# Two selective-scan layers of a Trainium2 kernel: another order of the four scan directions, the last image's norm cut into row blocks beside the last scans, part of the first image's convolution moved beside the first scans

## The chip, the cores and the metric

The kernel runs on one core of a Trainium2 chip. The metric is the device time of one execution in microseconds (us); the time before is the median of three runs. The names of the engines are those of the profile: PE is the matrix engine (PEld its weight loads), DVE the vector engine, ACT the scalar engine, POOL the GpSimd engine, SP the engine whose queue issues the DMAs.

## The reference, cut to what matters

Four layers work on 8 images of 48 x 48 pixels with 96 channels, each as `x = x + layer(groupnorm(x))`. The first and the last layer (L0 and L3) are the ones that the change touches. Both compute this:

```python
xz = x @ in_proj.T;  xc, z = split(xz)               # 2 x 192 channels
xc = silu(depthwise_conv3x3(xc))
xs = [rows forward, columns forward, rows backward, columns backward] of xc
for each of the 4 directions: dts, B, C = x_proj @ xs;  delta = softplus(dt_proj @ dts + bias)
    h = exp(delta * A) * h + (delta * u) * B          # 192 channels x 16 states, 2304 steps
    y = sum over the states of h * C + D * u
y = the four directions' y, put back to pixels and added
y = (y - mean) / sqrt(var + 1e-5) * norm_w + norm_b   # over the 192 channels of a pixel
out = (y * silu(z)) @ out_proj.T
```

A pixel's norm needs all four directions of that pixel, and nothing of other pixels. The second layer is a spectral filter with a small network, the third another scan layer; the change leaves their work as it is.

## The kernel before, in words

`ss2d` is one such layer. The 2304 pixels are cut into five blocks, `BLKS`: four of 10 rows (480 pixels) and one of 8 rows (384). In a column direction the same numbers mean columns. Its parts are, in order of the program:

* `load_x(0)`, `front(0)`, `conv(0)`: the first image is loaded into the padded tile `xpad`, normed, and convolved. `conv(b)` takes, for each block and each half of the 192 channels, nine matmuls from `xpad` into the PSUM tile of tag `side` (L481), one matmul for z into a PSUM tile of tag `s1` (L486), then two Silu activations on ACT (L490 into `us[b]`, L492), and stores z to `zs[b]` in DRAM (L494). Before the scans nothing lies beside it.
* `scans`: 8 images x 4 directions x 5 blocks. A block is four *turns*. A turn is three pairs of scans on DVE (L263), with what feeds and reads them: exp(delta A) by ACT into PSUM (L255), delta u B by DVE and POOL (L235), h C by POOL (L276, about 3 us each, twice a turn), and the sum over the states by PE (L296, L298, function `reduce`). Twice in a turn `aside(at)` issues work that belongs to something else: loads for the next block, one step of the generator `side`, and a step of `stage1`, which prepares the block two ahead (L593, L583, L587, L598, L611, and L422 on POOL). An image has 160 asides: 20 blocks x 4 turns x 2.
* `opening` and `done`: the sum of the four directions is held in `yss`. A block starts its PSUM accumulation with what is there and writes it back (ACT, L634).
* `side(job)`: during the scans of image `job` it issues, a step per aside, `load_x` of the next image, the norm of the last image, `post(job - 1)` (from the fourth aside on, for 52 asides), `front` of the next image, and from aside 80 on `conv(job + 1)`, 80 steps.
* `post(b)` first takes for all five blocks mean (PE, L504), difference (DVE, L507), square (ACT, L510), its sum (PE, L515) and a copy to `var` (DVE, L518); then one square root (ACT, L520) and one reciprocal (DVE, L522) over all; then for each block the loads of z and x (L528, L530), the factor spread over the channels (PE, L534), two products (DVE, L538), the product with z (POOL, L541), the output product (PE, L544 and L547), the sum (DVE, L550) and the store (L552). After the scans `post(nb - 1)` does it for the last image with nothing beside it.

Each engine takes its instructions in the order in which the program issues them; this order is written out by hand (`manual_schedule`), and the framework only adds the waits. The directions run in the order 0 to 3, where the last one, 3, goes over columns from behind:

```python
DIRS_SS = [(False, False), (True, False), (False, True), (True, True)]   # (columns, backward)
```

Of the kernel before, what the change touches and what calls it, by code (L numbers as in the profile page):

```python
# [9 lines left out]
F32 = mybir.dt.float32  # L10
AF = mybir.ActivationFunctionType
# [4 lines left out]
H, W, C = 48, 48, 96  # L16
L = H * W
DH = 96
NS = 16
NK = 4  # L20
# [4 lines left out]
BLKS = [(0, 10), (10, 10), (20, 10), (30, 10), (40, 8)]  # L25
BMAX = 480
WMAX = BMAX + 1
NG = 8
# [10 lines left out]
CH = 96  # L39
# [36 lines left out]
def vss_stack_kernel(ctx: ExitStack, tc: tile.TileContext, i: dict, out: bass.AP):  # L76
# [86 lines left out]
        yield  # L163


    def scans(dirs, restart, a, pools, ps, stage1, opening, done, side, tail):

# [3 lines left out]


        blocks = [Block(job, k, blk, n == 0, n == len(BLKS) - 1, dirs[k][1])
                  for job in range(nb) for k in range(NK)
                  for n, blk in enumerate(range(len(BLKS))[::-1 if dirs[k][1] else 1])]
        for b in blocks:
            b.columns(restart)
# [168 lines left out]
        for t, (b, q) in enumerate(turns):  # L348
            at, nblk = 2 * t, t // (NG // 2)
            if q == 0:  # L350
                if nblk + 2 < len(blocks):
                    plan(blocks[nblk + 2], at)
                if b.k == 0 and b.first:
                    beside = side(b.job)
            scan(t, 0)
            if t > 0:
                keep(t - 1, 1)
                make_hc(t - 1, 1)
            make_dbu(at + 2, nc.vector)
            make_da(t, 1)  # L360
            make_dbu(at + 3, nc.gpsimd)
            if t > 0:
                reduce(t - 1, 0)
            scan(t, 1)
            make_da(t, 2)
            copy_b(at + 3)
            make_dbu(at + 3, nc.vector)
            if t > 0:
                reduce(t - 1, 1)
            aside(at)  # L370
            bring(t + 1)
            keep(t, 0)
            make_hc(t, 0)
            make_da(t + 1, 0)
            scan(t, 2)
            copy_b(at + 4)
            finish(at + 1)
            aside(at + 1)
            if q == NG // 2 - 1 and b.k == NK - 1 and b.last:
                for _ in beside:  # L380
                    while tail:
                        tail.pop(0)()
# [47 lines left out]
    def ss2d(l, xin, xout, b0=0):  # L430
# [36 lines left out]
        def load_x(b):  # L467
            nc.sync.dma_start(xpad[:C, 1:1 + H, 1:1 + W], seq(xin[b], False))

        def conv(b):  # L470
            us[b] = big.tile([DH, 2, L], F32, tag="big", name="u")
            zs[b] = zdr.tile([DH, 2, L], F32, tag="z", name="zd")
            for r0, nr in BLKS:
                n = nr * SEG
                for half in range(2):
                    pu = side_psum()
                    for slot in range(7):
                        for tap in ((0,), (1, 2), (3,), (4, 5), (6,), (7, 8), ())[slot]:
                            dy, dx = tap // 3, tap % 3
                            at = (2 * tap + half) * DH  # L480
                            nc.tensor.matmul(pu[:, :n], lhsT=flat[:, at:at + P],  # L481
                                             rhs=xpad[:, r0 + dy:r0 + dy + nr, dx:dx + W],
                                             start=(tap == 0), stop=(tap == 8))
                        if slot == 6:
                            pz = ps("s1", 1)
                            nc.tensor.matmul(pz[:DH, :n], lhsT=w[f"{l}_in"][:, (2 + half) * DH:(3 + half) * DH],  # L486
                                             rhs=xpad[:C, 1 + r0:1 + r0 + nr, 1:1 + W], start=True, stop=True)
                        yield
                    s = slice(r0 * W, r0 * W + n)
                    nc.scalar.activation(us[b][:, half, s], pu[:DH, :n], AF.Silu, bias=w[f"{l}_cb"][:, half:half + 1])  # L490
                    z = zp.tile([DH, BMAX], F32, tag="z", name="z")
                    nc.scalar.activation(z[:, :n], pz[:DH, :n], AF.Silu)  # L492
                    yield
                    nc.sync.dma_start(zs[b][:, half, s], z[:, :n])  # L494

        def post(b):
            y = yss[b]
            var = small.tile([CH, L // CH], F32, tag="var", name="var")
            for r0, nr in BLKS:
                n = nr * SEG  # L500
                s = slice(r0 * W, r0 * W + n)
                pm = side_psum()
                for half in range(2):
                    nc.tensor.matmul(pm[:DH, :n], lhsT=mean, rhs=y[:, half, s], start=(half == 0), stop=(half == 1))  # L504
                yield
                yc = y[:, :, s]
                nc.vector.tensor_sub(yc, yc, pm[:DH, :n].unsqueeze(1).to_broadcast([DH, 2, n]))  # L507
                yield
                sq = lnp.tile([DH, 2, BMAX], F32, tag="sq", name="sq", bufs=1)
                nc.scalar.activation(sq[:, :, :n], yc, AF.Square)  # L510
                yield
                pv = side_psum()
                for c in range(n // CH):
                    for half in range(2):
                        nc.tensor.matmul(pv[:CH, c:c + 1], lhsT=sq[:, half, c * CH:(c + 1) * CH], rhs=ones,  # L515
                                         start=(half == 0), stop=(half == 1))
                yield
                nc.vector.tensor_copy(var[:, r0 * W // CH:(r0 * W + n) // CH], pv[:CH, :n // CH])  # L518
                yield
            nc.scalar.activation(var, var, AF.Sqrt, bias=eps5[:CH])  # L520
            yield
            nc.vector.reciprocal(var, var)  # L522
            yield
            for r0, nr in BLKS:
                n = nr * SEG
                s = slice(r0 * W, r0 * W + n)
                z = lnp.tile([DH, 2, BMAX], F32, tag="zin", name="zin", bufs=1)
                nc.sync.dma_start(z[:, :, :n], zs[b][:, :, s])  # L528
                xi = xio.tile([C, BMAX], F32, tag="xi", name="xi")
                nc.sync.dma_start(xi[:, :n], xin[b][:, s])  # L530
                pr = side_psum()
                for c in range(n // CH):
                    at = r0 * W // CH + c
                    nc.tensor.matmul(pr[:DH, c * CH:(c + 1) * CH], lhsT=var[:, at:at + 1].to_broadcast([CH, DH]),  # L534
                                     rhs=wc["ident"], start=True, stop=True)
                yield
                for half in range(2):
                    nc.vector.scalar_tensor_tensor(y[:, half, s], y[:, half, s], w[f"{l}_nw"][:, half:half + 1], pr[:DH, :n],  # L538
                                                   ALU.mult, ALU.mult)
                yield  # L540
                nc.gpsimd.tensor_mul(y[:, :, s], y[:, :, s], z[:, :, :n])  # L541
                po = side_psum()
                for half in range(2):
                    nc.tensor.matmul(po[:C, :n], lhsT=wnb[:, half, :], rhs=z[:, half, :n], start=(half == 0), stop=False)  # L544
                yield
                for half in range(2):
                    nc.tensor.matmul(po[:C, :n], lhsT=w[f"{l}_out"][:, half, :], rhs=y[:, half, s],  # L547
                                     start=False, stop=(half == 1))
                yield
                nc.vector.tensor_add(xi[:, :n], xi[:, :n], po[:C, :n])  # L550
                yield
                nc.sync.dma_start(xout[b][:, s], xi[:, :n])  # L552

        def side(job):
            used = 0
            more = job + 1 < nb
            if more:
                load_x(job + 1)
            if job > 0:

                for _ in range(3):
                    used += 1
                    yield
                for _ in post(job - 1):
                    used += 1
                    yield
            if more:
                for _ in front(job + 1):
                    used += 1
                    yield  # L570
                while used < 10 * NG:
                    used += 1
                    yield
                yield from conv(job + 1)

        def stage1(b):
            n = b.n
# [60 lines left out]
        load_x(0)  # L638
        for _ in front(0):
            pass  # L640
        for _ in conv(0):
            pass
        scans(dirs, False, a, pools, ps, stage1, opening, done, side, [])
        for _ in post(nb - 1):
            pass
        stack.close()

# [1 line left out]
    def lines(xin, xout):  # L649
# [169 lines left out]
        load_x(0)  # L819
        for _ in front(0):  # L820
            pass
        scans(dirs, True, a, pools, ps, stage1, opening, done, side, tail)
        stack.close()


# [286 lines left out]
```

## Time and profile before

| | us |
|---|---|
| median of 3 runs (19544.21 to 19555.11) | 19550.73 |
| the profiled execution | 19542.61 |
| its span, first to last instruction | 19540.6 |
| L0: start to the first scan | 148.7 |
| L0: after the last scan to the last sum of the norm | 5902.6 to 6007.1 |
| L3: start of the layer to its first scan | 13528.4 to 13675.7 |
| L3: after the last scan to the end | 19432.6 to 19540.6 |
| a 10-row block in L0 and L3 with nothing beside it | 34.5 to 34.8 |
| an 8-row block in L0 and L3 with nothing beside it | 29.5 to 31.5 |

A block's time is the distance from its first scan to the first scan of the next block, read from the scans (L263) in the trace's timeline of DVE. In the views, each row of a timeline has start, duration, engine, line, operation and operands, and in brackets how long the engine stood idle before it and for what. A windows view gives the busy time and the count of instructions of each engine in a stretch, the clock granted to PE as a share, the busy share of the DMA engines, and GB/s. All stretches of time are us from the start of the span.

### The profile page before, as it was taken

How to read it: one execution, taken by the hardware profiler on the slowest of the kernel's cores; microseconds unless marked ns; L12 is line 12 of the kernel's file. 1: busy time of each engine (PE TensorE's matmuls, PEld its weight loads, DVE VectorE, ACT ScalarE, POOL GpSimd, SP SyncE). 2: the span in 40 equal slices, each digit the busy share in tenths (PEclk: the TensorE clock that was granted, in tenths of full speed). 3: DMA queues.
4: the chain of work that ended last, by engine and by line, in shares of the span. 5: the costliest groups of instructions: out<-in, count | busy, mean ns of one | idle time of the engine just before them, and what ended most of it. 6: DMA issues, size and time to landing. Idle time of an engine off the chain costs nothing. (4 is left out here: it accounts for less than half of the span.)

```text
span 19540.6 us, 172984 instructions
## 1 busy us (share of the span) xinstructions
PE 15237.1 (78%) x53500; PEld 4370.8 (22%) x53500; DVE 16831.8 (86%) x11281; ACT 14144.5 (72%) x22222; POOL 16028.7 (82%) x9825
## 2 busy tenths in 40 slices
PE   6777777777767887888888988887677777777776
PEld 1211211211214552222222222222121121121121
DVE  6999999999992228999999999996999999999997
ACT  5877777877772227788788777885778778778775
POOL 6999999999991007888888888886999999999997
PEclk6777776776767777888878888887677677667765
DMA  3444444444443324434434444443444444444443
GB/s 130 160 162 158 162 160 163 158 163 158 156 170 48 50 45 145 145 141 150 150 139 147 147 146 145 144 149 112 158 163 160 159 164 157 160 162 161 156 165 123
DMA packets 768486, 2829.44 MB, mean 145 GB/s; under 512 B 235724, under 2 KB 298668, under 8 KB 640926
## 3 DMA queue, kind: packets, MB, share of 16 engines
q1 hardware_dynamic: 767558, 2818.38, 43.1%
q8 instruction: 422, 6.91, 0.1%
q14 instruction: 506, 4.15, 0.1%
HBM read 2371.42 MB, written 446.69 MB: 144 GB/s over the span
## 5 line engine op out<-in xcount | busy, mean ns | idle before, releaser
L263 DVE TENSOR_TENSOR_SCAN dbu<-ps_da,dbu 128x962 f32<-128x962 f32 (+3 forms) x5760 | 11858.2, 2071 | 897.9 <-ACT ps_da L255 895.7
L276 POOL TENSOR_TENSOR dbu<-dbu,bc 128x1440 f32<-128x1440 f32 (+1 forms) x3840 | 11439.8, 2985 | 1040.6 <-DVE dbu L263 814.0
L255 ACT ACTIVATE ps_da<-dd,w_l_a 128x481 f32<-128x481 f32 (+3 forms) x11520 | 7414.7, 648 | 2729.7 <-DVE dbu L263 2523.7
L296 PE MATMUL ps_y<-dbu,w_red 128*32 128x480 f32 (+1 forms) x23040 | 4983.6, 752 | 3051.0 <-POOL dbu L276 3047.3
L298 PE MATMUL ps_y<-dbu,w_red 128*32 128x480 f32 (+1 forms) x7680 | 4942.9, 752 | 0.0
L235 DVE TENSOR_TENSOR dbu<-dd,ps_b 128x1440 f32<-128x1440 f32 (+5 forms) x3840 | 4645.3, 1210 | 320.1 <-ACT ps_b L216 275.7
L235 POOL TENSOR_TENSOR dbu<-dd,bc 128x480 f32<-128x480 f32 (+3 forms) x1920 | 3026.2, 1576 | 61.9 <-DMA bc<-bcd 36.6
L296 PEld LDWEIGHTS ps_y<-dbu,w_red 128*32 128x32 f32 x23040 | 742.7, 125 | 7009.7 <-POOL dbu L276 5283.6
L216 ACT COPY ps_b<-bc 128x480 f32<-128x480 f32 (+1 forms) x3360 | 1798.4, 535 | 300.7 <-DVE dbu L235 271.3
L722 PE MATMUL ps_s<-xpad,w_l_cw 128*128 128x480 f32 (+1 forms) x2560 | 1747.2, 834 | 2.3 <-ACT xpad L124 1.6
L481 PE MATMUL ps_side<-xpad,w_l_cw 128*128 128x480 f32 (+1 forms) x2880 | 1617.4, 690 | 4.6 <-ACT xpad L124 4.5
L255 ACT ACT_TABLE_LOAD x970 | 1244.5, 1283 | 17.1
L113 POOL MEMSET w_l_cw<- 128x1760 f32 (+1 forms) x3 | 5.8, 1942 | 1326.7 <-DVE x L932 1321.3
L422 POOL TENSOR_TENSOR dds<-dds,u 96x480 f32<-96x480 f32 (+1 forms) x640 | 793.6, 1240 | 259.9 <-ACT dds L611 259.9
L593 PE MATMUL ps_s<-u,w_l_xp 96*38 96x480 f32 (+1 forms) x1280 | 957.2, 888 | 4.1 <-ACT dds L587 3.0
L583 PE MATMUL ps_s<-bcl,dtw 6*96 6x480 f32 (+1 forms) x1280 | 878.4, 775 | 86.3 <-ACT dds L587 82.2
L270 POOL COPY carry<-dbu 128x3 f32<-128x3 f32 x2048 | 386.4, 189 | 582.6 <-DVE dbu L263 570.2
L292 PE MATMUL ps_y<-ysum,w_ident 96*96 96x480 f32 (+1 forms) x960 | 740.7, 861 | 113.7 <-ACT ysum L634 112.8
L481 PEld LDWEIGHTS ps_side<-xpad,w_l_cw 128*128 128x128 f32 x2880 | 571.0, 222 | 1115.0 <-issue 916.4
L722 PEld LDWEIGHTS ps_s<-xpad,w_l_cw 128*128 128x128 f32 x2560 | 525.8, 210 | 1087.1 <-issue 938.1
L298 PEld LDWEIGHTS ps_y<-dbu,w_red 128*32 128x32 f32 x7680 | 683.1, 125 | 0.0
L763 PE MATMUL ps_s<-xpad,w_l_inz 96*96 96x480 f32 (+1 forms) x640 | 505.7, 924 | 86.9 <-ACT dds L757 69.2
(146 smaller groups left out, 12586.2 us busy)
## 6 DMA issues: line engine op xcount, KB each, us to landing
dd<-dd SPq DMA_DIRECT2D x512, 1443.0 KB
bc<-bcd SPq DMA_DIRECT2D x1536, 480.0 KB
dd<-dd SPq DMA_DIRECT2D x256, 1440.0 KB
dd<-dds SPq DMA_DIRECT2D x512, 360.8 KB
dd<-dd SPq DMA_DIRECT2D x128, 1155.0 KB
bc<-bcd SPq DMA_DIRECT2D x384, 384.0 KB
dd<-dds SPq DMA_DIRECT2D x256, 360.0 KB
dd<-dd SPq DMA_DIRECT2D x64, 1152.0 KB
```

What stands on the lines that cost most here:

```text
L216: nc.scalar.copy(bps[t][:, :b.n], bcs[t][:, 0, :b.n])
L235: engine.tensor_mul(o, du, by.unsqueeze(1).to_broadcast([P, hi - lo, b.n]))
L255: nc.scalar.activation(da[:, at:at + b.m], b.got[half][:, u % 3, 0, :], AF.Exp, scale=a[:, b.k, ci:ci + 1])
L263: nc.vector.tensor_tensor_scan(db, da, db, 0.0, ALU.mult, ALU.add)
L276: nc.gpsimd.tensor_mul(h, h, bcs.pop(2 * t + sub)[:, 1, :n].unsqueeze(1).to_broadcast([P, 3, n]))
L296: nc.tensor.matmul(y[32 * g:32 * g + 32, :n], lhsT=wc["red"][:, :32], rhs=hc[:, g, b.at], start=False, stop=(slot == 3))
L298: nc.tensor.matmul(y[DH:, :n], lhsT=wc["red"][:, 32:], rhs=hc[:, 2, b.at], start=(slot == 0), stop=(slot == 3))
L422: nc.gpsimd.tensor_mul(rows(du, n), rows(dt, n), u)
L481: nc.tensor.matmul(pu[:, :n], lhsT=flat[:, at:at + P], rhs=xpad[:, r0 + dy:r0 + dy + nr, dx:dx + W], start=(tap == 0), stop=(tap == 8))
L583: nc.tensor.matmul(got["p"][:DH, :n], lhsT=dtw[2 * NS:, b.k, half, :], rhs=b.bcl[2 * NS:, :n], start=True, stop=True)
L593: nc.tensor.matmul(got["p"][:NBC, :n], lhsT=w[f"{l}_xp"][:, b.k, half, :], rhs=u[:, half], start=(half == 0), stop=(half == 1))
L722: nc.tensor.matmul(got["u", half][:, :n], lhsT=flat[:, at:at + P], rhs=shifted(off), start=(tap == 0), stop=(tap == 3))
```

## The change

Four edits, all in the two layers of `ss2d`:

1. `scans` gets the order of the directions; `ss2d` gives (0, 1, 3, 2), so that the last direction goes over rows from behind and brings the row blocks to their final sum in the order 4, 3, 2, 1, 0. The third layer keeps its order.
2. Ahead of the scans only blocks 0 to 2 of the first image are convolved. Blocks 3 and 4 (18 of 48 rows) are issued by `side(0)` in asides 0 to 15, two steps an aside.
3. `load_x(1)` and `front(1)` come after these in `side(0)`, so from aside 16 on.
4. `post` takes a list of blocks. For the last image, `side(7)` issues blocks 4, 3, 2 and 1 one at a time, all steps of a block in six asides, two steps an aside, from asides 130, 138, 146 and 154 on. Block 0 follows after the scans. Each call has its own square root and reciprocal over its part of `var`.

```diff
-    def scans(dirs, restart, a, pools, ps, stage1, opening, done, side, tail):
+    def scans(dirs, order, restart, a, pools, ps, stage1, opening, done, side, tail):
-                  for job in range(nb) for k in range(NK)
+                  for job in range(nb) for k in order
-                if b.k == 0 and b.first:
+                if b.k == order[0] and b.first:
-            if q == NG // 2 - 1 and b.k == NK - 1 and b.last:
+            if q == NG // 2 - 1 and b.k == order[-1] and b.last:
-        def conv(b):
+        def conv(b, blks):
+            if blks[0] == BLKS[0]:
...
-        def post(b):
+        def post(b, blks=BLKS):
...
-            nc.scalar.activation(var, var, AF.Sqrt, bias=eps5[:CH])
+            nc.scalar.activation(var[:, v0:v1], var[:, v0:v1], AF.Sqrt, bias=eps5[:CH])
-            nc.vector.reciprocal(var, var)
+            nc.vector.reciprocal(var[:, v0:v1], var[:, v0:v1])
...
         def side(job):
             used = 0
             more = job + 1 < nb
+            if job == 0:
+                for n, _ in enumerate(conv(0, BLKS[3:])):
+                    if n % 2:
+                        used += 1
+                        yield
             if more:
                 load_x(job + 1)
...
-                yield from conv(job + 1)
+                yield from conv(job + 1, BLKS)
+            else:
+                for n, blk in enumerate(BLKS[:0:-1]):
+                    while used < (NK * len(BLKS) - len(BLKS) + n + 1) * NG + 2:
+                        used += 1
+                        yield
+                    for m, _ in enumerate(post(job, [blk])):
+                        if m % 2:
+                            used += 1
+                            yield
...
-        for _ in conv(0):
+        for _ in conv(0, BLKS[:3]):
             pass
-        scans(dirs, False, a, pools, ps, stage1, opening, done, side, [])
-        for _ in post(nb - 1):
+        scans(dirs, (0, 1, 3, 2), False, a, pools, ps, stage1, opening, done, side, [])
+        for _ in post(nb - 1, BLKS[:1]):
             pass
```

More of the change, by code (lines that the diff above doesn't have):

```diff
@@ L468, in load_x @@
             nc.sync.dma_start(xpad[:C, 1:1 + H, 1:1 + W], seq(xin[b], False))
-        def conv(b):
-            us[b] = big.tile([DH, 2, L], F32, tag="big", name="u")
-            zs[b] = zdr.tile([DH, 2, L], F32, tag="z", name="zd")
-            for r0, nr in BLKS:
+        def conv(b, blks):
+            if blks[0] == BLKS[0]:
+                us[b] = big.tile([DH, 2, L], F32, tag="big", name="u")
+                zs[b] = zdr.tile([DH, 2, L], F32, tag="z", name="zd")
+            for r0, nr in blks:
                 n = nr * SEG
@@ L494, in conv @@
                     nc.sync.dma_start(zs[b][:, half, s], z[:, :n])
-        def post(b):
+        def post(b, blks=BLKS):
             y = yss[b]
             var = small.tile([CH, L // CH], F32, tag="var", name="var")
-            for r0, nr in BLKS:
+            v0, v1 = min(r0 for r0, nr in blks) * W // CH, max(r0 + nr for r0, nr in blks) * W // CH
+            for r0, nr in blks:
                 n = nr * SEG
@@ L519, in post @@
                 yield
-            nc.scalar.activation(var, var, AF.Sqrt, bias=eps5[:CH])
+            nc.scalar.activation(var[:, v0:v1], var[:, v0:v1], AF.Sqrt, bias=eps5[:CH])
             yield
-            nc.vector.reciprocal(var, var)
+            nc.vector.reciprocal(var[:, v0:v1], var[:, v0:v1])
             yield
-            for r0, nr in BLKS:
+            for r0, nr in blks:
                 n = nr * SEG
@@ L821, in lines @@
             pass
-        scans(dirs, True, a, pools, ps, stage1, opening, done, side, tail)
+        scans(dirs, range(NK), True, a, pools, ps, stage1, opening, done, side, tail)
         stack.close()
```

## The prediction

> **What bounds the kernel now.** I began with the page's busy times to see which engines can be the limit.
>
> ```profile
> PE 15237.1 (78%) x53500; PEld 4370.8 (22%) x53500; DVE 16831.8 (86%) x11281; ACT 14144.5 (72%) x22222; POOL 16028.7 (82%) x9825
> ```
>
> DVE and POOL are both near full, and the shares are means over stages, so I went to the stages. The windows view of four stretches of L0 shows the inside of the scans: blocks 10 to 17 of image 0 (convolution beside them), the same blocks of image 7 (nothing beside), blocks 2 to 8 of image 0 (nothing) and of image 7 (the norm of image 6, from its fourteenth step on).
>
> ```profile
> 497.44:780.64 283.20, 219.39 (x764) 55.93 (x768) 262.03 (x160) 228.91 (x373) 262.75 (x182) 0.82 0.47 163
> 5567.86:5836.88 269.02, 178.10 (x600) 27.99 (x600) 261.57 (x161) 203.76 (x345) 260.62 (x181) 0.59 0.47 166
> 227.69:466.63 238.94, 163.38 (x528) 25.61 (x532) 232.88 (x141) 182.69 (x306) 227.96 (x159) 0.53 0.46 158
> 5282.73:5537.99 255.26, 190.31 (x684) 49.75 (x684) 244.39 (x162) 185.40 (x308) 239.03 (x166) 0.67 0.47 162
> ```
>
> With nothing beside, DVE and POOL are each busy 97% of the time: whatever makes either wait lengthens the scans. PE has room only while little lies beside it. The first two rows differ by 14.2 us, for seven half-blocks of convolution whose Silus fall among these scans: 2.0 us each.
>
> At both ends of the layer the scan engines stand still. The timeline of PE shows the convolution ahead of the scans; the last two halves of 10 rows are followed by two of 8 rows and then by the first work for the scans.
>
> ```profile
> 76.77 7.51 PE L481 MATMUL ps_side<-xpad,w_l_cw 128*128 128x480 f32 x18
> ...
> 105.94 0.81 PE L486 MATMUL ps_s<-xpad,w_l_in 96*96 96x384 f32 x2
> 107.33 1.80 PE L593 MATMUL ps_s<-u,w_l_xp 96*38 96x480 f32 x4 [0.58 <-ACT z L492]
> ```
>
> From 76.77 to 106.75 PE works on blocks 3 and 4, with only 0.58 us between the convolution and the next work. L3 is alike (13604.29 to 13634.27).
>
> The chain that ended last, in order of time, is the norm after the scans of L3:
>
> ```profile
> 19438.62 2.93 PE ps_side L504 x4
> 19441.57 1.16 DVE ysum L507
> 19442.76 1.01 ACT sq L510
> ...
> 19447.03 3.53 PE ps_side L504 x4
> ...
> 19484.00 1.90 PE ps_side L534 x10
> ...
> 19493.17 0.66 DVE xi L550
> ...
> 19494.34 4.16 DMA zin<-zd
> ...
> 19537.10 0.55 DVE xi L550
> ```
>
> One step follows another, on one engine at a time: the first phase takes 8.4 us for block 0 and the last sum ends at 19537.65, 99.0 us after the start. The same chain in L0 goes from 5908.56 to 6007.11, and the spectral stage's loads follow its last store on SP.
>
> **What the Trainium skill says.** "ScalarE: Activation LUTs", section "What ACT_TABLE_LOAD costs", gives 1283 ns for a load of a function's table, plus about 1380 ns of draining. The trace agrees on the load and shows no gap for the drain:
>
> ```profile
> 1289.16 1.28 ACT L490 ACT_TABLE_LOAD   x1
> 1290.45 0.66 ACT L490 ACTIVATE u<-ps_side,w_l_cb 96x480 f32<-96x480 f32 x1
> 1291.01 0.55 ACT L492 ACTIVATE z<-ps_s 96x480 f32<-96x480 f32 x1
> 1291.58 1.28 ACT L255 ACT_TABLE_LOAD   x1
> ```
>
> So a pair of Silus keeps ACT from the scans for 3.7 us, of which 2.0 us reach the turn: ACT has about 1.7 us of slack there. "TensorE: Matmul & The Clock Gate", section "What's actually happening", says that PE runs at half clock until it has been busy for some time. The trace agrees: a pass of 480 columns takes 0.80 us at the start of the convolution and 0.40 us from 29 us on, and the granted clock is 0.53 to 0.59 in bare scans and 0.82 with convolution beside. "Perfetto Trace Analysis", section "Tensor Engine Instruction (MATMUL, LD_WEIGHTS)", calls DVE, ACT and GpSimd strict first-in first-out; here too an instruction that waits keeps all behind it on its engine waiting, as the turn with the Silus shows, where the scans come late by ACT.
>
> **Part by part, for one layer.**
>
> *Convolution ahead of the scans:* 2 x 8.26 us (10 rows) and 2 x 6.74 us (8 rows) go: **30.0 us** saved. The rest of the start-up, from the first L593 to the first scan, stays.
>
> *Norm after the scans:* what stays is block 0: first phase 8.4, root and reciprocal 0.7 (19483.21 to 19483.87), second phase 9.8 (19484.00 to 19493.83), together 18.9 of 99.0 us; its z has landed long before, since no earlier block holds the buffer. **80.1 us** saved. The wait for PE's last reduce and the last store stay.
>
> *Four half-blocks of convolution beside the first two blocks of scans.* At the known density each costs 2.0 us, together 8.0. Here the density doubles. A block of scans with one half-block beside it keeps PE busy 219.39 / 8 = 27.4 us; another half-block adds 8.3 us at full clock, 35.7 us against a period of 34.6. PE is just full. What waits behind it: ACT's copy of B, C (L598) and dt activations (L587), in whose rear the next exponentials stand, for which DVE waits. Also the Silus now come in the same aside as their z matmul, and z shares its PSUM tile with `stage1`, whose next matmul (L583) waits for the Silu. SP's four z stores wait for nothing else. I take 2.0 us more per half-block, **16 us**. From below 8; from above 30, what PE takes for it by itself.
>
> *Load and norm of the second image.* This norm costs 41.6 + 37.4 - 2 x 34.6 = 9.8 us in blocks 0 and 1, and will cost that in blocks 2 to 4. But before, `load_x(1)` was issued at 135.75, ahead of the first scan. Now it and the first statistics on DVE lie in the same aside, and on SP it is behind the last Silu's z store. Image 1 has the same turn: the z store at 856.71, the load at 857.08, its last packet (transfer records of the trace) 7.1 us later at 864.2, while DVE comes to this place at 862.0. With the landing's notice, DVE stands **3 us**. From below 0 (part of the 9.8 may be start-up), from above 10 if SP comes late. The loads for the next blocks queue on SP behind it; the same load in image 1 leaves the turn after at 8.78, as in bare scans.
>
> *The order of the directions.* Costs nothing: in image 7 of L0 the bare 10-row blocks of the third and fourth directions take 34.5 to 34.8 us alike, in either column or row order; the two swap their places, and all transitions still need the whole previous direction.
>
> *Four blocks of norm beside the last direction.* The known price: blocks 0 to 6 of image 7 take 261.8 us (5207.11 to 5468.91, by their first scans). Bare they would take 239.0: blocks 2 to 6 of image 0 take 169.8, and 34.6 each is set for blocks 0 and 1. Less 2.0 for a last Silu, 21 us remain for five blocks, 4.2 each. Of this 3.6 us is DVE's own work (1.15 + 0.16 + 0.3 + 1.33 + 0.65). Now two steps share an aside. Places in a turn are from the turn that starts at 1298.97 in image 1:
> - mean and difference: DVE comes to the difference 6.8 us into its turn; PE has its last reduce done at 5.2 and the mean takes 1.9 to 3.5. Behind the waiting difference stands the third pair of scans, and POOL's h C behind that. With the difference itself 2.3 us.
> - copy and root: ACT waits for DVE, then 1.28 + 0.31 + 1.28 us; the next exponentials end some 2.2 us late. With copy and reciprocal 2.5 us. There are now four roots where there was one.
> - products and POOL's product: POOL would begin its h C at 6.1 us, but first waits for DVE's products (8.2 us) and works 2.2 us. In the next aside the output product waits for that, 2.3 to 3.5 us on PE, and DVE waits for the sum: done at 14.4 where the turn would be over at 8.7. 5.7 us.
>
> Together 10.5; I take **9.5 us** a block, since DVE's and POOL's delays partly cover each other: 38 us. From below 17 (4.2 each), from above 60 (15 each, most of the 18.9 that a block's chain takes alone). On SP the loads of z and x and the store stand ahead of loads that are not due for two asides.
>
> *Sum:* 30.0 + 80.1 - 16 - 3 - 38 = 53.1 us a layer, 106 us in both. The profiled execution took 19542.6 us (span 19540.6 and 2.0 around it) and becomes 19436.6; the median shown is 8.1 us above the profiled one, which gives **19445 us**.
>
> **The rivals.** *The covers hold:* density does not matter, the prices are 8 + 0 + 17 = 25 us. For it: most of the 4.2 us is DVE's bare work. Against it: POOL has 3% to spare. It gives 85 x 2 = 170 saved, 19381 us. *PE and POOL stall it more:* the upper prices, 30 + 10 + 60 = 100; for it the 5.78 us that ACT once waits for L593 behind an output product (1090.38 in image 1's timeline). It gives 20 saved, 19531 us. *It ends slower:* DVE twice per block stands until PE is through the reduces, which wait for POOL. Usually POOL is a few us behind, but the waits view has a longest wait of PE on L276 of 16.8 us. If each of the eight waits were that long, they cost 134 us; with 14 of work and 19 for the first image, the layer loses 57 us and the kernel 114: 19665 us. It decides from (110.1 - 19) / 4 = 22.8 us a block; one block's whole chain with nothing beside it takes 18.9, which speaks against it. *It does not do what it says:* if an access to one row block of the sum waited for the others of its tile, each block of norm would hold up the accumulation too. The trace of before has no such pair. It would add some 5 us a block, 40 in all: 19485 us.
>
> **How the numbers follow.** Forecast 0.57, covers hold 0.18, stalls 0.12, slower 0.04, false waits 0.09. About 0.2% (39 us) is what a measurement of this kernel can tell from no change. Faster by more: the forecast, the covers, the false waits and half of the stalls, 0.90; within it: the other half, 0.06; slower 0.04. The range goes from 19385, all but the best of the covers, to 19505, where the costs come to 87 us a layer; beyond lie most of the stalls and the slower case, under 2 in 10 with the lower end.
>
> **What would show it.** Right: the first scan at 118.7 us instead of 148.7; one pass of L504 to L552 after the last scan, some 20 us; blocks 0 and 1 of image 0 some 8 us longer than bare, with Silus at the ends of their second and fourth turns; a DVE wait of about 3 us for `xpad` at the start of block 2; blocks 16 to 19 of image 7 some 9 to 10 us longer each, the sum (L550) waiting for PE. Wrong: PE's clock at 0.5 and DVE waiting over 10 us a block in the first two blocks; row blocks of image 7's last direction over 50 us; blocks of other images changed by the new order.

## The result, and the profile after

The changed kernel takes 19447.19 us, the median of 4 runs (19445.46 to 19450.70), against 19552.92 us in 4 runs of the kernel before beside it. The ratio is 0.9945 with a 95% interval of 0.9928 to 0.9962: 106 us faster, with an interval clear of 1. The forecast was 19445 us. The profiled execution took 19445.46 us, its span 19443.7 us.

The busy line of the page of the changed kernel hardly differs from that before: DVE's busy time is the same to 2 us and POOL's to 10 us, PE is busy 31 us less and ACT 46 us more. What was gained is time in which the scan engines stood.

```profile
PE 15206.3 (78%) x53500; PEld 4384.0 (23%) x53500; DVE 16830.2 (87%) x11289; ACT 14190.2 (73%) x22262; POOL 16019.2 (82%) x9825
```

The sum over both layers, read from the first and last scans (L263) of each stage in the two profiled executions, is this. A minus is time saved.

| part | forecast, both layers | measured, both layers |
|---|---|---|
| convolution ahead of the scans | -60.0 | -57.8 (29.1 and 28.7) |
| norm after the scans | -160.2 | -152.9 (76.3 and 76.6) |
| first image: convolution, load and norm beside the scans | +38 | +16.0 |
| last image: four blocks of norm beside the scans | +76 | +69.4 |
| order of the directions, all images | 0 | +20 |
| sum | -106 | -105 |

In the rows of the first and the last image 1.2 us an image is taken off for the order and counted in the row of the order: in images 1 to 6, where only the order differs, the layers are longer by 6.9 us (L0) and 8.2 us (L3) together, about 1.25 us an image, so 20 us for all 16. The spans themselves differ by 96.9 us; the other 8.4 us lie in the spectral stage (17.4 us longer) and in the third layer (9.0 us shorter), whose code is the same. Over the profiles of this study these two stages vary from 1390 to 1408 us and from 6092 to 6121 us, so that part is scatter between executions.

**Ahead of the scans.** The timeline of PE of the changed kernel has, after the second half of block 2, the first work for the scans where block 3's convolution stood before:

```profile
77.24 0.97 PE L487 MATMUL ps_s<-xpad,w_l_in 96*96 96x480 f32 x2
78.87 1.80 PE L611 MATMUL ps_s<-u,w_l_xp 96*38 96x480 f32 x4 [0.66 <-ACT z L493]
```

L611 (L593 before) begins at 78.87 instead of 107.33 us. The timeline of DVE shows the first scan:

```profile
119.61 2.16 DVE L263 TENSOR_TENSOR_SCAN dbu<-ps_da,dbu 128x962 f32<-128x962 f32 x1 [3.43 <-ACT ps_da L255]
```

It was at 148.7 us.

**Beside the scans.** The windows view of the changed kernel has here the first two blocks of image 0, with the four half-blocks of convolution (a sixth of whose matmuls runs before the first scan), and blocks 16 to 19 of image 7 up to the end of the last scan, with the four blocks of norm. The columns are those of the forecast's windows: the stretch, its length, the busy time of PE, PEld, DVE, ACT and POOL with counts, PE's granted clock, the DMA share and GB/s.

```profile
119.61:193.46 73.85, 54.46 (x202) 18.75 (x206) 68.77 (x41) 61.54 (x97) 60.11 (x44) 0.84 0.46 153
5756.70:5926.16 169.46, 120.51 (x438) 37.50 (x438) 146.02 (x101) 106.27 (x171) 135.82 (x85) 0.62 0.35 117
```

The same view of the kernel before, for blocks 16 to 19 of image 7, with nothing beside:

```profile
5767.29:5902.60 135.31, 80.43 (x280) 11.58 (x280) 134.22 (x78) 94.63 (x155) 131.16 (x82) 0.57 0.37 131
```

The first stretch is 4.4 us longer than two bare blocks of 34.7 us, and PE is busy 27.2 us a block in it, 74% of the time. The four norm blocks lengthen their stretch by 34.1 us (169.46 less 135.31). DVE's own work grows by 11.8 us; its idle time grows from 1.1 to 23.4 us. Two thirds of the price are waits.

**After the scans.** The chain of the changed kernel, in order of time, is now one pass over block 0:

```profile
19410.40 2.21 POOL ysum L544
19412.61 6.04 POOL dbu L276 x2
...
19419.88 3.46 PE ps_side L507 x4
19423.36 1.16 DVE ysum L510
19424.54 1.01 ACT sq L513
19425.60 3.37 PE ps_side L518 x20
...
19436.70 3.21 PE ps_side L550 x4
19439.94 0.65 DVE xi L553
```

The mean L507 (L504 before) begins 7.5 us after the last scan's end at 19412.34, where it was 6.0 us before: the last h C (L276) on POOL now stands behind the product with z of block 1 (L544). From there to the end of the sum it takes 20.7 us where there were 99.0.

### The profile page after: what moved, and what is told of

Same layout as the page of the kernel before. It is cut to its first block, busy times and chain, and to the rows that moved or that the text cites. A ratio compares the mean times of both kernels' runs of the same rounds, so it can differ in the third digit from the quotient of the medians.

```text
span 19443.7 us, 172969 instructions
## 1 busy us (share of the span) xinstructions
PE 15206.3 (78%) x53500; PEld 4384.0 (23%) x53500; DVE 16830.2 (87%) x11289; ACT 14190.2 (73%) x22262; POOL 16019.2 (82%) x9825
## 4 chain that ended last, share of the span: by engine, by line
DVE 32%; PE 19%; POOL 16%; ACT 15%; issue 13%; DMA 5%; SPq 0%; POOLq 0%; DVEq 0%; ACTq 0%
DVE dbu L263 20%; POOL dbu L276 12%; DVE dbu L235 11%; ACT ps_da L255 4%; PE ps_s L740 3%; ACT L255 3%; PE ps_y L296 3%; DMA dd<-dd 2%; PE ps_h L970 2%; POOL dds L422 2%; PE ps_s L611 2%; PE ps_y L983 2%; PE ps_s L812 1%; POOL dbu L235 1%; PE ps_side L482 1%
## 5 line engine op out<-in xcount | busy, mean ns | idle before, releaser
L263 DVE TENSOR_TENSOR_SCAN dbu<-ps_da,dbu 128x962 f32<-128x962 f32 (+3 forms) x5760 | 11853.3, 2070 | 927.4 <-ACT ps_da L255 925.1
L276 POOL TENSOR_TENSOR dbu<-dbu,bc 128x1440 f32<-128x1440 f32 (+1 forms) x3840 | 11433.5, 2984 | 1051.2 <-DVE dbu L263 837.5
L601 PE MATMUL ps_s<-bcl,dtw 6*96 6x480 f32 (+1 forms) x1280 | 880.6, 777 | 90.7 <-ACT dds L605 80.9
L611 PE MATMUL ps_s<-u,w_l_xp 96*38 96x480 f32 (+1 forms) x1280 | 931.7, 867 | 2.8 <-ACT dds L605 1.5
L292 PE MATMUL ps_y<-ysum,w_ident 96*96 96x480 f32 (+1 forms) x960 | 747.5, 868 | 114.1 <-ACT ysum L652 112.6
L768 PE MATMUL ps_s<-bcl,dtw 6*96 6x480 f32 (+1 forms) x640 | 424.1, 799 | 181.7 <-ACT bcl L762 181.7
```

Of the source, the lines that this page charges most:

```text
L263: nc.vector.tensor_tensor_scan(db, da, db, 0.0, ALU.mult, ALU.add)
L276: nc.gpsimd.tensor_mul(h, h, bcs.pop(2 * t + sub)[:, 1, :n].unsqueeze(1).to_broadcast([P, 3, n]))
L601: nc.tensor.matmul(got["p"][:DH, :n], lhsT=dtw[2 * NS:, b.k, half, :], rhs=b.bcl[2 * NS:, :n], start=True, stop=True)
L611: nc.tensor.matmul(got["p"][:NBC, :n], lhsT=w[f"{l}_xp"][:, b.k, half, :], rhs=u[:, half], start=(half == 0), stop=(half == 1))
```

## The experiments

Each ratio is to runs of the kernel before on the same chip (median 19548.83 us of 24 runs for the first four, 19553.25 us of 17 runs for the others).

### The order of the directions alone

```diff
-        scans(dirs, False, a, pools, ps, stage1, opening, done, side, [])
+        scans(dirs, (0, 1, 3, 2), False, a, pools, ps, stage1, opening, done, side, [])
```

All else is as before.

> The kernel before with the order of directions (0, 1, 3, 2) alone; convolution and norm as before. My theory, from the traces of before and after: in images 1 to 6, where only the order differs, an image takes 1.2 us longer, at blocks 9 and 10, less 0.8 at block 15, because a column direction's product of delta and u on POOL (L422) takes 1.2 to 1.45 us where a row direction's takes 1.0 to 1.2, and the short blocks 9 and 10 don't hide it. 16 images: 15 to 20 us longer than before. Rival, the prediction's: the order costs nothing, 0 us, and the 1.2 us come from the moved work shifting the phase of the queues.

Measured: 19564.83 us (13 runs), ratio 1.0008, interval 1.0000 to 1.0016, so +16 us with an interval that just touches zero. The profiled execution has its scans of L0 10.8 us and of L3 7.7 us longer than before. Block by block it is small and much alike in images 0, 3 and 7, which I compared: the last block of the second direction and the first of the third are longer by 0.9 to 1.8 us together, and the first of the fourth is shorter by up to 1.0; most other blocks stay within 0.1 us, with single ones up to 0.9. The forecast's "costs nothing" falls.

### The convolution moved, alone

```diff
-        for _ in conv(0):
+        for _ in conv(0, BLKS[:3]):
+            if job == 0:
+                for n, _ in enumerate(conv(0, BLKS[3:])):
+                    if n % 2:
+                        used += 1
+                        yield
```

The order is (0, 1, 2, 3), and the whole norm of the last image is after the scans.

> The kernel before with the convolution of the first image cut 3 to 2 alone; order and norm as before. Theory from the trace of after: 29 us a layer saved ahead of the scans, image 0 some 7.5 us longer (four Silu pairs at 0.2 to 2.1 us, 3 us for the load of the second image), so 21 us a layer and 42 us in all saved. Rival, the prediction's step: 30 saved and 19 lost, 11 a layer, 22 us in all.

Measured: 19503.03 us (12 runs), ratio 0.9978, interval 0.9969 to 0.9986: 46 us faster. By the forecast's steps it would have been 22 (60.0 less twice 19). In the profiled execution the first scans come 29.6 and 30.3 us earlier than before, and image 0 is only 6.5 and 8.3 us longer. The moved convolution was priced too high.

### The order and the norm by blocks, without the convolution

```diff
+                for n, blk in enumerate(BLKS[:0:-1]):
...
-        for _ in post(nb - 1):
+        for _ in post(nb - 1, BLKS[:1]):
```

The convolution of the first image is whole and ahead of the scans.

> The kernel before with the order and the last image's norm by blocks, convolution as before. Theory: 76.5 us a layer saved after the scans, 34 to 36 lost in image 7, 8 lost by the order, so 33 a layer and 66 us in all; together with the convolution alone it makes up the whole change (sum of both near 106). Rival: the two parts help each other or stand in each other's way, and the sum differs from the whole by over 15 us.

Measured: 19478.85 us (5 runs), ratio 0.9963, interval 0.9950 to 0.9975: 70 us faster. Image 7 is 37.3 and 34.8 us longer and its blocks 16 to 19 take, to 0.1 us, what they take in the whole change: the two parts do not act on each other. Their gains add up to 116 us where the whole gives 106, with intervals that reach 17, 24 and 33 us to either side (convolution, norm, whole).

### The same norm, eight asides a block instead of six

```diff
-                        if m % 2:
+                        if m in (0, 2, 3, 5, 7, 9, 10, 11):
```

This separates steps that wait for each other: mean and difference, the square and its sum, and the output product and the sum with x no longer share an aside. The products on DVE and POOL's product still do.

> The changed kernel with the twelve steps of each block of norm spread over eight asides instead of six, so that no engine is asked for a result in the aside that starts it: mean | difference, square | sum of squares | copy, root | reciprocal, factor | products, POOL's product | output product | sum. Theory: of the 12 us that a block of norm costs now, 3.8 are DVE's wait for the mean and 3.9 its wait for the output product; both go, blocks 17 and 18 lose 6 to 8 us each, 20 to 24 us a layer, 40 to 48 us in all. Rival: POOL is the bound, its 2.2 us and the wait for the products stay, and the waits only move to other turns: under 10 us in all.

Measured: 19412.54 us (5 runs), ratio 0.9929, interval 0.9917 to 0.9942, 34 us below the median of the whole change (31 us by the two ratios). Image 7 costs 23.8 and 21.2 us instead of 37.2 and 34.6: 13.4 us a layer came back, more than the rival gave and less than the theory's 40 in both. The timeline of DVE in block 17 tells which wait went:

```profile
5814.42 1.15 DVE L510 TENSOR_TENSOR ysum<-ysum,ps_side 96x960 f32<-96x960 f32 x1 [0.67 <-PE ps_side L507]
```

The difference waits 0.67 us for the mean, where it waited 3.84. The windows view of this kernel, over the same blocks to 3.5 us past the last scan, still has DVE idle for 13.6 us, 2.1 of them after the last scan:

```profile
5756.63:5916.50 159.87, 117.11 (x437) 37.39 (x438) 146.28 (x101) 105.88 (x171) 139.12 (x86) 0.63 0.37 124
```

So 11.5 us of idle time are left beside the scans against 23.4 with six asides: the waits are fewer, not gone. One of those left is that for the output product, which has moved into the first turn of the next block (10.5 us in block 17 where 8.3 is bare).

### An empty step or three between the load and the statistics

```diff
             if more:
                 load_x(job + 1)
+            if job == 0:
+                for _ in range(3):
+                    used += 1
+                    yield
```

> The changed kernel with three empty asides between the load of the second image and its norm, as the other images have them. Theory: the 3.05 us for which DVE stands for xpad at the first statistics go, block 2 of image 0 takes 3 us less and nothing comes back later: image 0 takes 3 us less in each of the two layers. Rival: the wait only covers for ACT, which is late by the last Silu pair; then DVE waits for the exponentials instead and image 0 stays within 1 us.

Measured in one run: 19417.2 us. That is 30 us below the changed kernel, but in the profiles most of the difference lies in the spectral stage and the third layer, which no edit touched; only the blocks count here. Image 0 is 5.7 and 5.9 us longer than before instead of 8.6 and 9.8. In the changed kernel the timeline of SP has the last Silu's z store and the load of the second image one after the other,

```profile
196.19 0.33 SPq L495 DMA_DIRECT2D zd<-z  x1
196.62 0.67 SPq L468 DMA_DIRECT2D xpad<-in_x_dram  x1
```

and the timeline of DVE the statistics that wait for it:

```profile
204.63 1.02 DVE L138 BATCH_NORM_STATS2 st<-xpad 96x6 f32<-96x384 f32 x2 [3.05 <-DMA xpad<-in_x_dram]
```

In the timeline of DVE of the experiment they start without a wait:

```profile
211.59 0.99 DVE L138 BATCH_NORM_STATS2 st<-xpad 96x6 f32<-96x384 f32 x2
```

The wait of 3.05 us was forecast as 3 us, and it is about what the pause gives back (2.9 us in L0; 3.9 in L3, where the wait is 3.45 us).

### The square root left out of the single blocks

```diff
-            nc.scalar.activation(var[:, v0:v1], var[:, v0:v1], AF.Sqrt, bias=eps5[:CH])
+            if len(blks) > 1:
+                nc.scalar.activation(var[:, v0:v1], var[:, v0:v1], AF.Sqrt, bias=eps5[:CH])
```

This leaves out a part of the computation, the square root of the variance for all five blocks of the last image. With it go two table loads per block on ACT.

> The changed kernel with the square root left out of the five single-block calls of the norm (their variances are inverted as they are), so without its activation and the two table loads around it. Theory: the third turn of blocks 16 to 19 of image 7 (10.0, 10.0, 9.5, 9.5 us) falls to some 8.5 us, 1.0 to 1.6 us less each, 5 to 6 us a layer. Rival: DVE's waits of that turn are for PE; it stays within 0.3 us.

Measured in one run: 19433.01 us. The third turns of blocks 16 to 19, in which DVE waited for the exponentials behind the root, fall from 10.0, 10.0, 9.5 and 9.5 to 8.4 us, near the bare 8.3. That is 5.4 us together, and image 7 costs 6.0 us less in L0 and 5.7 in L3: a root costs some 1.4 to 1.5 us. The second and fourth turns, those of the mean and of the output product, become shorter in block 17 (by 1.9 and 1.7 us) and longer in block 18 (by 1.1 and 1.5), so these waits move between blocks when the root is gone and stay nearly the same in sum.

### Another order that also ends with rows backward

```diff
+        scans(dirs, (0, 3, 1, 2), False, a, pools, ps, stage1, opening, done, side, [])
```

All else is as before. The two column directions meet at column block 0, of 10 columns, instead of block 4, of 8.

> The kernel before with the order (0, 3, 1, 2) alone, which also ends with backward rows. POOL's product of delta and u takes 2.89 us per block for columns and 2.24 for rows, whatever the order; what differs is how many of the four short blocks have columns to prepare: two in the kernel before, three with (0, 1, 3, 2), two again here. Theory: no slower than the kernel before, 0 us within 4 (scans of images 1 to 6 within 0.4 us an image). Rival: two column directions in a row, or columns straight before backward rows, cost something by themselves; then 1.2 us an image and 15 to 20 us stay.

Measured: 19538.70 us (13 runs), ratio 0.9993, interval 0.9985 to 1.0001: no slower than the kernel before, and below the first order, whose interval begins where this one ends. The scans of L0 take 5753.0 us and those of L3 5752.6 (before 5753.9 and 5756.9). What cost 16 us is therefore not that the layer ends with rows backward, but how the other directions follow each other. The count of short blocks that have columns to prepare (two before, three in the first order, two here), which the expectation gave as the cause, fits both orders; it was tested in no other way. By what instruction the block at that seam gets longer was not settled.

### All three improvements together

The changed kernel with the eight asides, the pause of three asides and the order (0, 3, 1, 2), each edit as shown above.

> The changed kernel with the norm's steps over eight asides, the pause before the second image's norm and the order (0, 3, 1, 2). If the parts add: 27 to 34 us below the changed kernel by the steps, 6 by the pause, 16 to 20 by the order, so 50 to 60 us below it and 150 to 165 us below the kernel before. If the order's gain does not hold with the norm beside it: 130 to 145 us below the kernel before.

Measured: 19365.31 us (4 runs), ratio 0.9903, interval 0.9888 to 0.9918: 188 us below the kernel before and 82 below the changed one. Image 0 costs 2.2 and 2.4 us, image 7 19.2 and 19.3 us, and the scans of L0 take 5776.1 us where the changed kernel needs 5806.6. This is more than was expected, 50 to 60 us below the changed kernel. By the blocks, the asides gave 27 us, the pause 7 and the order should give about 20, together 54; both layers' scans account for 63 (30.5 and 32.7). The rest, some 19 us, lies outside the scans that were edited and is of the size of the scatter named above. What is left to gain is in the timeline of DVE of this kernel, in block 17 and the turn after it:

```profile
5796.66 1.15 DVE L510 TENSOR_TENSOR ysum<-ysum,ps_side 96x960 f32<-96x960 f32 x1 [0.65 <-PE ps_side L507]
...
5810.72 2.16 DVE L263 TENSOR_TENSOR_SCAN dbu<-ps_da,dbu 128x962 f32<-128x962 f32 x1 [0.94 <-ACT ps_da L255]
...
5829.56 0.65 DVE L553 TENSOR_TENSOR xi<-xi,ps_side 96x480 f32<-96x480 f32 x1 [3.61 <-PE ps_side L550]
```

The sum still waits 3.61 us for the output product.

## Why the prediction was right, and which of its steps were not

The forecast of 106 us saved was met, and by the mechanism that it named: two stretches in which one engine worked at a time went under the scans, and came back in part as longer turns. But two of its steps were off by about 20 us each, in opposite directions, and cancelled. That the total came out at the very number was in part luck.

**Convolution ahead of the scans: right.** 30.0 us a layer were forecast, 29.1 and 28.7 came; 29.6 and 30.3 in the experiment with this part alone.

**Four half-blocks of convolution: the step "PE is just full" failed.** It added a half-block at full clock, 8.3 us, to the 27.4 us of a block with one half-block, got 35.7 us against a period of 34.6, and took 2.0 us more per half-block, 16 us together. The window of the first two blocks has PE busy for only 27.2 us a block. Most of the gap is work that the sum counted and that is not there. In the forecast's windows a bare block holds 75 instructions of PE and a block with one half-block 95.5, so a block with two would hold some 115; here there are 101. The timeline of PE has some of the missing ones ahead of the first scan, just after PE stood idle for 12.9 us:

```profile
106.47 4.53 PE L482 MATMUL ps_side<-xpad,w_l_cw 128*128 128x480 f32 x6
110.92 1.80 PE L611 MATMUL ps_s<-u,w_l_xp 96*38 96x480 f32 x4
112.66 2.68 PE L482 MATMUL ps_side<-xpad,w_l_cw 128*128 128x480 f32 x6
```

These 9.0 us are 12 of the 72 instructions of the moved convolution and the first step of `stage1` for a later block. Two of the four half-blocks also have 8 rows, 6.74 us by the forecast's own figure and not 8.3. By estimate the two make up 6 of the 8.5 us a block by which the sum was too high ((9.0 + 2 x 1.5) / 2). The busy time of the scans' own matmuls is no constant either. The timeline of PE shows the same group of reduces with much beside it and with little:

```profile
187.39 0.60 PE L296 MATMUL ps_y<-dbu,w_red 128*32 128x480 f32 x3
197.57 1.02 PE L296 MATMUL ps_y<-dbu,w_red 128*32 128x480 f32 x3 [3.45 <-POOL dbu L276]
```

The Trainium skill, "TensorE: Matmul & The Clock Gate", section "What's actually happening", says that PE is throttled by default and that activity releases it; here the granted clock is 0.53 to 0.59 in bare scans and 0.84 in this window. But the forecast's 27.4 us were already taken at 0.82, so between these two windows the clock explains little. What stayed is what the Silus cost: the turns that carry them are longer by 2.1, 2.0, 0.2 and about 2.0 us, so some 6 us for the four, below the forecast's own lower end of 8. The one Silu pair at 0.2 us was not followed further.

**Load and norm of the second image: right.** DVE's wait for `xpad` was to be 3 us and is 3.05; the pause removes it.

**The order of the directions: "costs nothing" failed.** It rested on blocks of the two directions taking the same time when bare. The blocks do; the seams between the directions do not. Alone it costs 16 us by the runs, 18.5 by the scans of the profiled execution. The forecast compared the inside of the directions and put the transitions at zero because they wait for the same things.

**Norm after the scans: right but for its size.** 80.1 us a layer were forecast, 76.3 and 76.6 came. The term that was off is "what stays, 18.9 us", which is 20.7, and "the wait for PE's last reduce stays", which grew by 1.5 us because POOL's product for block 1 comes ahead of the last h C. The 1.8 us lie on PE: in its timeline, the mean, the sum of the squares and the output product of block 0 take 3.5, 3.4 and 3.4 us where they took 3.0, 3.0 and 2.5.

**Four blocks of norm beside the scans: the sum nearly right, the parts not.** Forecast were 9.5 us each, 38 together; blocks 16 to 19 are longer by 7.8, 11.9, 10.9 and 3.5 us, 34.1 together, in L0 and, to 0.1 us, in L3. The timeline of DVE in block 17 has the three places that the forecast named, in its order:

```profile
5818.23 1.15 DVE L510 TENSOR_TENSOR ysum<-ysum,ps_side 96x960 f32<-96x960 f32 x1 [3.84 <-PE ps_side L507]
...
5831.42 2.16 DVE L263 TENSOR_TENSOR_SCAN dbu<-ps_da,dbu 128x962 f32<-128x962 f32 x1 [1.53 <-ACT ps_da L255]
...
5845.43 0.65 DVE L553 TENSOR_TENSOR xi<-xi,ps_side 96x480 f32<-96x480 f32 x1 [3.88 <-PE ps_side L550]
```

*Mean and difference,* forecast at 2.3 us, make the second turn 5.0 us longer. Here the working took the end of PE's last reduce, 5.2 us into the turn, from a turn in image 1. In block 17 the turn begins at 5807.59, and the timeline of PE shows what stands ahead of the mean:

```profile
5805.84 3.42 PE L611 MATMUL ps_s<-u,w_l_xp 96*38 96x480 f32 x4
5809.19 1.92 PE L292 MATMUL ps_y<-ysum,w_ident 96*96 96x480 f32 x2
5811.04 1.02 PE L296 MATMUL ps_y<-dbu,w_red 128*32 128x480 f32 x3
...
5813.68 1.02 PE L296 MATMUL ps_y<-dbu,w_red 128*32 128x480 f32 x3 [0.81 <-POOL dbu L276]
...
5814.48 1.02 PE L296 MATMUL ps_y<-dbu,w_red 128*32 128x480 f32 x3
...
5815.44 2.76 PE L507 MATMUL ps_side<-ysum,mean 96*96 96x480 f32 x4
```

The last two groups of reduces wait for POOL, whose h C ends 6.0 us into the turn, and take 1.02 us each instead of 0.60, so the mean starts 7.8 us into the turn. In the turn of image 1 POOL was through at 4.2 us; DVE had just stood 1.9 us for a Silu there, in which POOL could catch up (that this is why was not tested). The kernel before has POOL through at 6.2 us in the second turn of its bare block 17. So the place was read from a turn that is not like these: some 1.8 us of the error are POOL's, some 0.9 PE's, which runs at a granted clock of 0.62 here. *Copy and root,* forecast at 2.5, cost 1.8 in this block and about 1.5 by the experiment without the root. *The products and POOL's product,* forecast at 5.7, cost 5.2: POOL's L544 takes its 2.21 us ahead of h C, and DVE's sum waits 3.88 us for L550. Over the four blocks the second turns are longer by 13.3 us where these parts give 9.2, the third by 5.9 for 10.0, and the fourth by 15.0 for 22.8.

Block 19, for which the forecast took the same 9.5, costs 3.5. Its output product falls after the scans, and its difference has no wait at all. That `stage1` has nothing left to prepare is not enough for this, since block 18 has no L611 on PE either and its difference still waits:

```profile
5864.51 1.15 DVE L510 TENSOR_TENSOR ysum<-ysum,ps_side 96x960 f32<-96x960 f32 x1 [3.41 <-PE ps_side L507]
```

In block 19 POOL's h C is done 3.6 us into the second turn instead of 4.8, and the mean takes PE 1.85 us instead of 3.51.

So of the rivals, "the covers hold" was wrong by the norm blocks and right about the convolution; "PE and POOL stall it more", "it ends slower" and the false waits on the tile are shown by nothing: the longest wait of DVE in these four blocks is 3.9 us, not 16.8; the opening matmul of the accumulation (L292) waits for ACT's write-back (L652) and never for an instruction of the norm; and the first turns of blocks 17 to 19, each with a block of norm just ahead, are at the bare 8.3 us.

## What to carry to other kernels

A stretch at the end of a stage in which one engine waits for the next is worth cutting into pieces that can go under the work ahead of it, even when that work keeps its engines 97% busy: of 153 us saved after the scans only 69 came back here. Where the pieces are put decides how much comes back: a step and the step that waits for it should not share a slot on an in-order engine, and one slot between them took a wait of 3.84 us to 0.67, though the same did not remove the wait for the output product (3.61 us). When work is added to PE, first count where its matmuls will run, and do not add its duration to a busy time measured at another granted clock.

## What the runs showed of the hardware that was not expected

* Added matmuls shorten those that were there. In the forecast's windows of blocks 10 to 17, PE is busy 22.3 us a block with nothing beside at a granted clock of 0.59, and 27.4 us with one half-block of convolution at 0.82: 5.2 us more, where the half-block takes 8.26 us ahead of the scans.
* The same code varies between executions by more than the parts that were disputed here. The spectral stage, which no edit touched, took between 1390 and 1408 us, while most blocks of scans repeat to 0.1 us, and single ones to 1 us. A part of 10 us was read from its own blocks and not from the end-to-end time.
* POOL's product over columns is slower than over rows. The timeline of POOL, in the third direction of image 7, has for the changed kernel, which prepares a column direction there,

```profile
5554.83 1.44 POOL L422 TENSOR_TENSOR dds<-dds,u 96x480 f32<-96x480 f32 x1
5560.34 1.45 POOL L422 TENSOR_TENSOR dds<-dds,u 96x480 f32<-96x480 f32 x1
```

and for the kernel before, which prepares rows in the same place,

```profile
5565.95 1.20 POOL L422 TENSOR_TENSOR dds<-dds,u 96x480 f32<-96x480 f32 x1
5571.23 1.04 POOL L422 TENSOR_TENSOR dds<-dds,u 96x480 f32<-96x480 f32 x1
```

That is 2.89 against 2.24 us for a block's two products. It is the same sum in any order of the directions, so it does not by itself explain the 16 us of the order; whether it matters at the seam stays open.
